# A 3x3 convolution computed by pairs of columns inside a fused convolution-and-attention kernel

## The chip, the cores and the metric

The kernel runs on one core of one Trainium2 chip. The core has five engines that run their own instruction streams: TensorE (PE in the profile; its weight loads are listed apart as PEld), VectorE (DVE), ScalarE (ACT), GpSimd (POOL) and SyncE (SP), which here only issues DMAs. Engines wait for each other through semaphores; each works through its own stream in order. The metric is the device time of one execution in microseconds (us); less is better.

## The reference, cut to what matters

Input x is 8 images of 32 x 32 positions with 256 channels, all in float32. The first layer is a group norm, then a 3x3 convolution to 192 channels beside an 8-head attention with relative positions to 64 channels. The second layer is a one-head attention over the 1024 positions and then a feed-forward part with two of eight experts per image.

```python
x = x + _L0_conv_ref(_gn(x), ...)            # 3x3 convolution (192) | attention (64)
t = _to_tokens(x)                            # (8, 1024, 256)
t = t + _L1_attn_ref(_ln_t(t), ...)          # one-head attention
t = t + _L1_ffn_ref(_ln_t(t), ...)           # top-2 of 8 experts
...
conv_out = lax.conv_general_dilated(x, conv_w, window_strides=(1, 1), padding='SAME', ...) + conv_b
```

Per image the convolution is, for each position, a sum over 3 rows and 3 columns of taps and 256 input channels.

## The kernel before

**Stages.** The program has two parts. The first (all but the last function body) goes through the 8 images and does layer 0 and the attention of layer 1; the second does the experts. One image of the first part takes about 270 us and has these stages, in TensorE's order, which is written out by hand (`tc.manual_schedule` for PE; the other engines' order is made by the scheduler of the language from priorities and dependencies):

- *Fill.* `input_steps(b + 1)` makes the next image's queries, keys, values and tables of relative positions from its normed image: products pk (L303), values pvv (L336), and 16 "small" steps of prel (L371 and L374). It is a generator; `attention_layer(b)` calls `fill` between its own steps, and `fill` runs four products of the next image's convolution behind each small step. `whole` then runs on to the end of a group.
- *Layer 1 attention* of image b: pq, lg1, tp, po1, pa1 (L673 to L759), and at its end, on GpSimd, a sum over the tokens (L793, L795) and the store of the image to DRAM (L800).
- *Score stage* of image b + 1 (`conv_layer_attention`, its first ten steps, s = 0 to 9). Each step has two scores: PE makes lg (L472), VectorE reduces it (L480), and after each second step L484 and L487 follow on VectorE. Between them stands the rest of the convolution (`conv.run(todo)`), and the generator `between`, which loads the image after (L104, on GpSimd's queue), turns it by PE (tpx, L245), copies it (L247) and takes its statistics (L248) on VectorE, adds biases on GpSimd (L252), and prepares the group norm (pm L256, pv L265). The normed image goes into `gpad` (L273).
- *Weighing stage*: scores of the later units beside exponentials (L512 on PE, L520 on ScalarE) and weighted sums po (L528). There is no convolution in it.

**The convolution** (`conv_steps`, L410 to L428). The normed image lies in `gpad` three times, shifted by one column to either side (L279 and L280 on GpSimd), with rows of zeros above and below, so that 128 positions (four rows of 32) of any tap are one contiguous piece. A tile t of 128 positions is one group of 18 products: 9 taps by 2 halves of the channels, accumulated in one PSUM bank and then added into the residual tile T by one VectorE operation (L427).

```python
lhsT=gflat[:, dx, kc, t * P + dy * WW : (t + 1) * P + dy * WW],
rhs=convw[:, i, :],
```

The bank is one of three `st` banks in the score stage, which tpx, pm, pmx and pv use too, and the only `po` bank in the fill (`place`).

An image has 8 groups, 144 products. Of these 64 run in the fill, 8 in `whole`, and 72 in the score stage (18 at its start, then 6 or 5 per step). Image 0 has no fill before it, so all its 144 run in its score stage (18, then 13 or 12 per step).

**Tokens.** T holds positions t x 128 + p in partition p, tile t; images are read, stored and written in this layout. The values of the attention lie in `v32`, 32 columns for each head (8 values, a one, and zeros).

Of the kernel before, what the change touches and what calls it, by code (L numbers as in the profile page):

```python
# [35 lines left out]
def kernel(  # L36
# [54 lines left out]
    with ExitStack() as ph:  # L91
# [9 lines left out]

        def load_image(b):
            t = work.tile([P, NT, C], FP, tag="T", name="T", bufs=2)
            nc.gpsimd.dma_start(out=t, in_=xt[b].rearrange("(t p) c -> p t c", p=P))  # L104
            return t
# [15 lines left out]
        convw = wp.tile([P, 9 * KC, CO], FP, tag="convw", name="convw")  # L121
        nc.scalar.dma_start(out=convw, in_=conv_w.rearrange("a b (k p) o -> p (a b k) o", p=P))
# [94 lines left out]

        tab = wp.tile([P, 1], FP, tag="tab", name="tab")
        v32 = wp.tile([P, NT, NH, 32], FP, tag="v32", name="v32")
        nc.gpsimd.memset(v32, 0.0)  # L220
        nc.gpsimd.memset(v32[:, :, :, DH : DH + 1], 1.0)


        gpad = wp.tile([P, 3, KC, HH + 2, WW], FP, tag="gpad", name="gpad")
        nc.gpsimd.memset(gpad, 0.0)
        gflat = gpad.rearrange("p s k h w -> p s k (h w)")
# [8 lines left out]
        def norm_steps(b):  # L235


# [3 lines left out]
            for kc in range(KC):  # L241
                for q in range(2):
                    tp = st_tile("tpx").rearrange("p (j t) -> p j t", j=4)
                    for j in range(4):
                        nc.tensor.transpose(tp[:, j, :], T[b][:, q * 4 + j, kc * P : (kc + 1) * P], ident)  # L245
                    dst = xT[:, kc, q * 512 : (q + 1) * 512]
                    nc.vector.tensor_copy(dst, tp.rearrange("p j t -> p (j t)"))  # L247
                    nc.vector.bn_stats(st[:, kc, q, :], dst)  # L248
                    yield True
                nc.vector.bn_aggr(mv[:, kc, :], st[:, kc].rearrange("p q s -> p (q s)"))  # L250
# [19 lines left out]
            yield None  # L270
            for kc in range(KC):
                xv = xT[:, kc, :].rearrange("p (h w) -> p h w", w=WW)
                nc.vector.tensor_scalar(  # L273
                    gpad[:, 1, kc, 1 : HH + 1, :], xv, gm[:, kc, :], gr[:, kc : kc + 1], ALU.subtract, ALU.mult
                )

            for kc in range(KC):
                mid = gpad[:, 1, kc, 1 : HH + 1]
                nc.gpsimd.tensor_copy(gpad[:, 0, kc, 1 : HH + 1, 1:WW], mid[:, :, 0 : WW - 1])  # L279
                nc.gpsimd.tensor_copy(gpad[:, 2, kc, 1 : HH + 1, 0 : WW - 1], mid[:, :, 1:WW])  # L280

        def by_tiles():
# [3 lines left out]
            for kc in range(KC):  # L286
                for a in range(2):
                    for e in range(4):
                        nc.gpsimd.tensor_copy(
                            xn[:, kc, a * 4 + e].rearrange("p (y x) -> p x y", y=8),  # L290
                            gpad[:, 1, kc, 1 + 16 * a : 17 + 16 * a, 8 * e : 8 * e + 8],
# [3 lines left out]
        def input_steps(b, held):  # L295
# [4 lines left out]
            for q in range(2):  # L300
                pk = st_tile("pk")
                for kc in range(KC):
# [3 lines left out]
                        rhs=gflat[:, 1, kc, WW + 512 * q : WW + 512 * (q + 1)],  # L306
# [27 lines left out]
            for j in range(NT):  # L334
# [10 lines left out]
                v32[:, :, :, 0:DH],  # L345
# [65 lines left out]
        def conv_steps(b, place):  # L411

            n = 9 * KC
            for t in range(NT):
                pc = place[0]("pc")
                for i in range(n):
                    tap, kc = divmod(i, KC)
                    dy, dx = divmod(tap, 3)
                    nc.tensor.matmul(  # L419
                        pc[:, 0:CO],  # L420
                        lhsT=gflat[:, dx, kc, t * P + dy * WW : (t + 1) * P + dy * WW],
                        rhs=convw[:, i, :],
                        start=i == 0,
                        stop=i == n - 1,
                    )
                    if i == n - 1:
                        nc.vector.tensor_tensor(T[b][:, t, 0:CO], pc[:, 0:CO], T[b][:, t, 0:CO], ALU.add)  # L427
                    yield  # L428

        class Unit:  # L430
# [91 lines left out]
            def gather(self, j, parts):  # L522
# [4 lines left out]
                for hl in range(HG):  # L527
                    nc.tensor.matmul(  # L528
                        self.po[32 * hl : 32 * hl + 32, cols],
                        lhsT=v32[:, j, self.g * HG + hl, :],  # L530
# [12 lines left out]
            def close(self):  # L543
                self.os = work.tile([P, 512], FP, tag="os", name="os")
                nc.scalar.copy(self.os, self.po)  # L545
# [21 lines left out]
        def conv_layer_attention(b, units, kq, rh, rwd, rwq, conv, between):  # L567
# [8 lines left out]
            first = min(left, 9 * KC)  # L576
            conv.run(first)
            left -= first
            for s in range(NU * NT + lead + 2):
# [34 lines left out]
                elif s == lead:  # L614
                    for _ in between:
                        pass
                if s % NT == 0 and 0 < u <= NU:
# [197 lines left out]
        class Conv:  # L815


            def __init__(self, b):
                self.place = [po_tile]
                self.steps = conv_steps(b, self.place)  # L820
                self.left = NT * 9 * KC if b < B else 0
# [7 lines left out]
            def whole(self):  # L829

                self.run(self.left % (9 * KC))

        with tc.manual_schedule(engines={mybir.EngineType.PE}):
            held = {}
            for _ in norm_steps(0):
                pass
            held["xn"] = by_tiles()
# [4 lines left out]
            for b in range(B):  # L842
                last = b + 1 == B
                def between():
                    if not last:
                        T[b + 1] = load_image(b + 1)
                    yield True
                    norm = iter(()) if last else norm_steps(b + 1)
                    while next(norm, None):
                        yield True  # L850
                    if means:
                        token_mean(*means.pop())
                    yield None
                    yield from norm

                conv.place[0] = st_tile
                conv_layer_attention(b, *(held[k] for k in ("units", "kq", "rh", "rwd", "rwq")), conv, between())
# [5 lines left out]
                def fill(us):  # L863

                    while us > 0:
# [4 lines left out]
                        if small:  # L870
                            conv.run(4)
# [156 lines left out]
    for b in range(B):  # L1028
# [22 lines left out]
        for q in range(2):  # L1051
# [34 lines left out]
            for j in range(4):  # L1086
# [5 lines left out]
                out=ot[b, q * 512 : (q + 1) * 512, :].rearrange("(t p) c -> p t c", p=P), in_=y  # L1092
# [51 lines left out]
```

## Time and profile before

| what | value |
|---|---|
| median of 3 runs | 2748.75 us (2745.79 to 2751.4) |
| profiled execution, its own time | 2752.85 us |
| span of the profiled execution, first to last instruction | 2750.8 us |
| mean granted TensorE clock | 0.970 |
| score stage of image 0, first product of the convolution to the first weighing matmul | 81.93 to 147.87 us |
| fill of image 2, first pk to the first pq | 531.06 to 581.65 us |
| score stage of image 2, first product of the convolution to the first weighing matmul | 634.21 to 686.09 us |
| load of an image, issue to landing, median of 8 | 6.3 us |

The profile is of one execution. Its page lists for each engine the busy time and its share of the span, then groups of instructions by line, engine and tile names (out<-in), with count, busy time, mean duration in ns, and the idle time of the engine just before them with what released it. A float32 matmul leaves two records, so counts of PE are twice those of the code. A timeline line gives start, length, engine, line, operation, tiles and, in brackets, how long the engine had been idle before and what ended that wait. A table by stretches gives busy times of PE, PEld, DVE, ACT and POOL in each stretch, then the granted clock (1.00 is full speed), the share of DMA and GB/s.

### The profile page before, as it was taken

The page shows a single profiled execution, that of the slowest core. Times are in us where ns is not written, and L with a number is a line of the kernel's source. Part 1 is how long each engine was busy: PE and PEld are TensorE (multiplying, and loading weights), DVE is VectorE, ACT ScalarE, POOL GpSimd, SP SyncE. Part 2 cuts the span into 40 slices and gives each one's busy share as a digit, 9 for nine tenths or more (in the row PEclk, how much of TensorE's full clock was granted, in tenths as well). Part 3 has the DMA queues.
Part 4 walks back from the last instruction along what each step waited for, and adds up shares of the span by engine and source line. Part 5 has one row for each costly group of instructions (what it writes and reads, how often), then busy time and mean ns, then how long its engine had stood idle before and what let it go on. Part 6 is the DMA issues. An engine that isn't in the chain of part 4 may idle for free.

```text
span 2750.8 us, 41933 instructions
## 1 busy us (share of the span) xinstructions
PE 2584.5 (94%) x17513; PEld 1541.4 (56%) x17513; DVE 1372.2 (50%) x2423; ACT 956.0 (35%) x1600; POOL 393.9 (14%) x440
## 2 busy tenths in 40 slices
PE   3999999999999999999999999999999859999998
PEld 2844763476347635753575367537742536666665
DVE  3474377337733773377237724862484443223332
ACT  0055215521552154315431633263336313222222
POOL 5010121002100301030103010201100131111110
PEclk9899999999999899999999999999999979999999
DMA  2330133023302320232023103320330032211110
GB/s 75 78 64 5 42 68 65 6 47 72 56 6 47 80 46 6 47 86 42 21 44 81 34 21 64 60 35 20 75 59 10 1 111 69 69 62 61 62 54 23
DMA packets 77611, 135.83 MB, mean 49 GB/s; under 512 B 12000, under 2 KB 32360, under 8 KB 75376
## 3 DMA queue, kind: packets, MB, share of 16 engines
q1 hardware_dynamic: 71504, 114.42, 19.3%
q0 software_dynamic: 3328, 16.78, 1.9%
q8 instruction: 138, 2.26, 0.3%
q10 hardware_dynamic: 2592, 1.97, 0.2%
q14 instruction: 49, 0.40, 0.1%
HBM read 53.43 MB, written 25.17 MB: 29 GB/s over the span
## 4 chain that ended last, share of the span: by engine, by line
PE 82%; DVE 8%; POOL 3%; DMA 3%; ACT 3%; issue 1%; ACTq 0%; DVEq 0%; SPq 0%; POOLq 0%
PE lg L472 13%; PE pc L419 11%; PE po L528 9%; PE py L1075 8%; PE phd L1057 8%; PE st L512 7%; PE po L741 4%; PE lg L710 3%; PE prel L371 3%; PE pq L673 2%; PE tp L730 2%; DVE my L480 2%; PE py L1072 1%; PE prel L374 1%; POOL part L793 1%; DMA T<-in_x_dram 1%
## 5 line engine op out<-in xcount | busy, mean ns | idle before, releaser
L480 DVE TENSOR_REDUCE my<-lg 128x32 f32<-128x1024 f32 x512 | 616.2, 1221 | 168.8 <-PE st L512 124.9
L520 ACT ACTIVATE PT<-st 128x512 f32<-128x512 f32 (+1 forms) x944 | 543.3, 633 | 340.7 <-PE st L512 332.7
L512 PE MATMUL st<-F,km 32*128 32x512 f32 x2048 | 549.1, 651 | 15.9 <-DMA F<-mb 15.7
L472 PE MATMUL lg<-km,F 24*128 24x512 f32 x2048 | 526.8, 656 | 1.3 <-DVE my L480 1.2
L419 PE MATMUL pc<-convw,gpad 128*128 128x192 f32 x2304 | 445.5, 343 | 6.3 <-DVE T L427 6.3
L419 PEld LDWEIGHTS pc<-convw,gpad 128*128 128x128 f32 x2304 | 381.2, 195 | 80.8 <-issue 65.1
L528 PE MATMUL po<-PT,v 128*32 128x256 f32 (+1 forms) x3200 | 314.5, 454 | 5.0 <-ACT os L545 2.6
L472 PEld LDWEIGHTS lg<-km,F 24*128 24x128 f32 x2048 | 156.1, 189 | 168.0 <-issue 105.6
L528 PEld LDWEIGHTS po<-PT,v 128*32 128x32 f32 x3200 | 67.4, 108 | 316.2 <-issue 281.5
L1075 PE MATMUL py<-w,hT 128*128 128x256 f32 x1024 | 237.3, 385 | 0.0
L512 PEld LDWEIGHTS st<-F,km 32*128 32x128 f32 x2048 | 178.2, 187 | 102.5 <-issue 64.5
L1057 PE MATMUL phd<-n2T,w 128*128 128x512 f32 x512 | 223.4, 594 | 0.0
L1075 PEld LDWEIGHTS py<-w,hT 128*128 128x128 f32 x1024 | 190.3, 190 | 45.3 <-issue 22.4
L1082 DVE TENSOR_TENSOR r<-py,n 128x256 f32<-128x256 f32 x64 | 27.2, 425 | 310.8 <-PE py L1075 310.8
L1057 PEld LDWEIGHTS phd<-n2T,w 128*128 128x128 f32 x512 | 97.0, 191 | 114.6 <-issue 107.5
L658 POOL TENSOR_TENSOR T<-T,n 128x256 f32<-128x256 f32 x64 | 47.0, 740 | 640.7 <-DVE n L653 640.7
L268 ACT ACTIVATE gr<-gr 128x2 f32<-128x2 f32 x8 | 1.6, 204 | 387.3 <-DVE gr L267 387.3
L741 PE MATMUL po<-pt,qkv 128*128 128x256 f32 x512 | 116.6, 381 | 11.3 <-DVE pt L733 11.3
L1064 ACT ACTIVATE hT<-phd,b1c 128x512 f32<-128x512 f32 x128 | 86.3, 686 | 96.3 <-PE phd L1057 96.1
L710 PE MATMUL lg<-qkv 128*128 128x512 f32 x256 | 119.1, 593 | 0.0
L741 PEld LDWEIGHTS po<-pt,qkv 128*128 128x128 f32 x512 | 96.8, 190 | 36.1 <-DVE pt L733 13.2
L719 DVE TENSOR_REDUCE nm<-lg 128x1 f32<-128x1024 f32 x64 | 78.1, 1220 | 72.5 <-PE lg L710 72.5
(220 smaller groups left out, 2456.5 us busy)
## 6 DMA issues: line engine op xcount, KB each, us to landing
F<-rh SPq DMA_DIRECT2D x256, 128.0 KB
F<-kq SPq DMA_DIRECT2D x256, 64.0 KB
F<-rwd SPq DMA_DIRECT2D x256, 64.0 KB
w<-in_L_ffn_W_dram SPq DMA_DIRECT2D x32, 512.0 KB
T<-in_x_dram POOLq DMA_DIRECT2D x8, 1024.0 KB, 6.3
rwd<-rw SPq DMA_DIRECT2D x16, 512.0 KB
Td<-T POOLq DMA_DIRECT2D x8, 1024.0 KB, 7.6
T<-Td SPq DMA_DIRECT2D x8, 1024.0 KB
```

The costliest lines, as they stand in the source:

```text
L371: nc.tensor.matmul(dst, lhsT=lhsT, rhs=kqv[rows, :, a], start=True, stop=True)
L419: nc.tensor.matmul(pc[:, 0:CO], lhsT=gflat[:, dx, kc, t * P + dy * WW : (t + 1) * P + dy * WW], rhs=convw[:, i, :], start=i == 0, stop=i = ...
L472: nc.tensor.matmul(lg[:, a, :], lhsT=self.F[r : r + 24, a, 0, i * P : (i + 1) * P], rhs=KM[self.g][r : r + 24, a].rearrange("p e k -> p (e ...
L480: nc.vector.tensor_reduce(my[:, :, hl], lg.rearrange("p a (y x) -> p y a x", y=WW), AX.XY, ALU.max)
L512: nc.tensor.matmul(st[:, i, :] if len(heads) > 1 else st, lhsT=KM[self.g][r : r + 32, a, e, :], rhs=self.F[r : r + 32, a, e, :], start=Tru ...
L520: nc.scalar.activation(self.pts[j][:, hs, :], st, AF.Exp)
L528: nc.tensor.matmul(self.po[32 * hl : 32 * hl + 32, cols], lhsT=v32[:, j, self.g * HG + hl, :], rhs=self.pts[j][:, hl, cols], start=j == 0, ...
L710: nc.tensor.matmul(lg[:, h, :], lhsT=qk[0][:, i * P : (i + 1) * P], rhs=qk[1][:, h * 512 : (h + 1) * 512], start=True, stop=True,)
L741: nc.tensor.matmul(po[:, 0:IB], lhsT=v1[:, jc, :], rhs=pt[:, jc, :], start=jc == 0, stop=jc == NT - 1)
L1057: nc.tensor.matmul(phd, lhsT=ws[k][0][:, kc, f * P : (f + 1) * P], rhs=n2T[:, kc, q * 512 : (q + 1) * 512], start=kc == 0, stop=kc == KC - 1,)
L1064: nc.scalar.activation(hT[:, k * NF + f, :], phd, AF.Gelu, bias=b1c[:, f, k * B + b : k * B + b + 1])
L1075: nc.tensor.matmul(py, lhsT=hT[:, k * NF + f, j * P : (j + 1) * P], rhs=ws[k][1][:, f, :], start=False, stop=k == TOPK - 1 and f == NF - 1,)
```

## The change

Two neighbouring columns of the output, with taps w0, w1, w2 and inputs d0 to d3, are (d0 w0 + d1 w1 + d2 w2) and (d1 w0 + d2 w1 + d3 w2): six products. They are computed from four: m0 = (d1 + d2)(w0 + w2 + w1)/2, m1 = (d2 - d1)(w0 + w2 - w1)/2, m2 = (d0 - d2) w0 and m3 = (d1 - d3)(-w2). The first column is m0 + m1 + m2 and the second m0 - m1 + m3, as the kernel has its signs.

- **Taps.** The taps are loaded into a work tile, and VectorE (four operations) and ScalarE (two) make the four sets `convw` from them once, at the start.
- **Inputs.** `gpad` is now one image with a border on all sides. A new function `by_pairs` makes the four sets `gdif` of sums and differences, 16 pairs by 34 rows each, by eight GpSimd operations of 512 elements; they take the place of the four shifted copies. It is called where the score stage ends (`behind()`, s = lead), and before `by_tiles` for image 0. The norm into `gpad` itself moves before the token mean, out of the last call of `between`.
- **Products.** A group is now one pair of sets (m0 and m1, or m2 and m3) of 128 pairs of columns (eight rows): 2 x 6 products of the same shape, 192 columns. An image has 8 groups, 96 products. The fill runs three behind each small step (48), `whole` finds nothing left to do, and 48 stand in the score stage: 12 at its start, then 4 or 3 per step. Image 0 has 12, then 9 or 8 per step.
- **Evictions.** An even group is added to T by three VectorE operations, an odd group by one of 384 elements.
- **Layout of T.** A residual tile now holds the even or the odd columns of eight rows, so two tokens that follow each other share a partition, and loads and final stores move 2 KB in one piece. The copies xT (now on ScalarE, before on VectorE) and os put tokens back in order.
- **Values.** `vall` packs 9 columns per head; a head's weight tile of 32 columns runs into the next heads' columns.

```diff
-            nc.gpsimd.dma_start(out=t, in_=xt[b].rearrange("(t p) c -> p t c", p=P))
+            nc.gpsimd.dma_start(out=t.rearrange("p (r j) c -> p r j c", j=2), in_=xt[b].rearrange("(r p j) c -> p r j c", p=P, j=2))
...
+        nc.vector.tensor_tensor(convw[:, 2], taps[:, 0], taps[:, 2], ALU.add)
+        nc.vector.tensor_tensor(convw[:, 0], convw[:, 2], taps[:, 1], ALU.add)
+        nc.vector.tensor_tensor(convw[:, 1], convw[:, 2], taps[:, 1], ALU.subtract)
+        nc.vector.tensor_scalar(convw[:, 0:2], convw[:, 0:2], 0.5, None, ALU.mult)
+        nc.scalar.copy(convw[:, 2], taps[:, 0])
+        nc.scalar.mul(convw[:, 3], taps[:, 2], -1.0)
...
-        v32 = wp.tile([P, NT, NH, 32], FP, tag="v32", name="v32")
-        nc.gpsimd.memset(v32, 0.0)
-        nc.gpsimd.memset(v32[:, :, :, DH : DH + 1], 1.0)
+        vall = wp.tile([P, NT, (NH - 1) * (DH + 1) + 32], FP, tag="vall", name="vall")
+        nc.gpsimd.memset(vall, 1.0)
...
-        gpad = wp.tile([P, 3, KC, HH + 2, WW], FP, tag="gpad", name="gpad")
+        gpad = wp.tile([P, KC, HH + 2, WW + 2], FP, tag="gpad", name="gpad")
         nc.gpsimd.memset(gpad, 0.0)
+        gdif = wp.tile([P, 4, KC, HH + 2, WW // 2], FP, tag="gdif", name="gdif")
+        nc.gpsimd.memset(gdif, 0.0)
...
-                    nc.vector.tensor_copy(dst, tp.rearrange("p j t -> p (j t)"))
+                    nc.scalar.copy(
+                        dst.rearrange("p (r t j) -> p r j t", r=2, j=2), tp.rearrange("p (r j) t -> p r j t", j=2)
+                    )
...
+        def by_pairs():
             for kc in range(KC):
-                mid = gpad[:, 1, kc, 1 : HH + 1]
-                nc.gpsimd.tensor_copy(gpad[:, 0, kc, 1 : HH + 1, 1:WW], mid[:, :, 0 : WW - 1])
-                nc.gpsimd.tensor_copy(gpad[:, 2, kc, 1 : HH + 1, 0 : WW - 1], mid[:, :, 1:WW])
+                d = [gpad[:, kc, 1 : HH + 1, j : j + WW - 1 : 2] for j in range(4)]
+                for v, (one, two, op) in enumerate(
+                    ((1, 2, ALU.add), (2, 1, ALU.subtract), (0, 2, ALU.subtract), (1, 3, ALU.subtract))
+                ):
+                    nc.gpsimd.tensor_tensor(gdif[:, v, kc, 1 : HH + 1, :], d[one], d[two], op)
...
+            n = 3 * KC
+            for r in range(NT // 2):
+                both = T[b][:, 2 * r : 2 * r + 2, 0:CO]
+                for pair in range(2):
+                    pc = place[0]("pc")[:, 0 : 2 * CO].rearrange("p (v o) -> p v o", v=2)
+                    for v in range(2):
+                        for i in range(n):
+                            dy, kc = divmod(i, KC)
+                            at = (8 * r + dy) * (WW // 2)
+                            nc.tensor.matmul(
+                                pc[:, v, :],
+                                lhsT=gflat[:, 2 * pair + v, kc, at : at + P],
+                                rhs=convw[:, 2 * pair + v, dy, kc, :],
+                                start=i == 0,
+                                stop=i == n - 1,
+                            )
+                            if v and i == n - 1:
+                                if pair:
+                                    nc.vector.tensor_tensor(both, pc, both, ALU.add)
+                                else:
+                                    nc.vector.tensor_tensor(
+                                        both, both, pc[:, 0:1, :].to_broadcast([P, 2, CO]), ALU.add
+                                    )
+                                    for j, op in enumerate((ALU.add, ALU.subtract)):
+                                        nc.vector.tensor_tensor(both[:, j], both[:, j], pc[:, 1, :], op)
+                            yield
...
                 elif s == lead:
                     for _ in between:
                         pass
+                    behind()
...
-                            conv.run(4)
+                            conv.run(3)
```

## The prediction

> **What bounds the kernel now.** I read the page's parts 1 and 5 first, then the list of what each engine waited for, then TensorE, VectorE, GpSimd and queue timelines of one image (image 2, counted from 0: 531 to 801 us), then tables by stretch of time.
>
> The page says that TensorE (PE) is busy 94% of the span and that the convolution's products are its fifth heaviest group:
>
> ```profile
> PE 2584.5 (94%) x17513; PEld 1541.4 (56%) x17513; DVE 1372.2 (50%) x2423; ACT 956.0 (35%) x1600; POOL 393.9 (14%) x440
> ...
> L419 PE MATMUL pc<-convw,gpad 128*128 128x192 f32 x2304 | 445.5, 343 | 6.3 <-DVE T L427 6.3
> ```
>
> One matmul leaves two records, so 2304 records are 1152 products (144 per image, 8 images). Back to back one costs 5.85/18 = 0.325 us (36 records in 5.85 us in the chain of work); a run of four after another kind costs 1.50. After the change there are 96 per image. "94% busy" says that 48 products x 8 images x 0.325 = 125 us come off; I don't believe it, because the products stand in two different stages. From the table by stretches (columns: length, busy us of PE, its weight loads, VectorE, ScalarE, GpSimd, then the granted clock):
>
> ```profile
> 531.00:582.00 51.00, 50.10 (x595) 43.50 (x594) 15.14 (x39) 8.91 (x14) 10.39 (x9) 1.00 0.08 27
> ...
> 634.00:657.40 23.40, 22.82 (x137) 17.42 (x135) 16.11 (x25) 0.70 (x2) 13.95 (x17) 1.00 0.63 151
> 657.40:688.00 30.60, 27.00 (x131) 18.35 (x134) 26.73 (x41) 1.49 (x2) 4.83 (x2) 0.80 0.11 24
> ```
>
> In the first stretch ("fill": the next image's convolution between small matmuls of layer 1) PE is the only full engine. The other two are the "score" stage (20 reduces, the rest of the convolution, the next image's norm). After 657.4 VectorE is full (26.7 of 30.6), PE waits, and its clock falls to 0.80. The timelines show why:
>
> ```profile
> 657.38 0.66 PE L245 MATMUL tpx<-ident,T 128*128 128x128 f32 x4 [0.58 <-DMA T<-in_x_dram]
> ...
> 676.78 0.58 PE L256 MATMUL pm<-gmv,gavg 128*128 128x2 f32 x2 [3.58 <-DVE gmv L250]
> ```
> ```profile
> 667.79 2.34 DVE L480 TENSOR_REDUCE my<-lg 128x32 f32<-128x1024 f32 x2
> 670.16 4.30 DVE L484 TENSOR_TENSOR my<-my,rwq 128x128 f32<-128x128 f32 x1
> ```
> ```profile
> 669.82 4.49 POOL L252 TENSOR_TENSOR T<-T,l0b 128x2048 f32<-128x2048 f32 x1 [18.20 <-PE tpx L245]
> ```
> ```profile
> 672.00:675.00 3.00, 1.20 (x8) 0.90 (x6) 2.93 (x4) 0.00 (x0) 2.31 (x1) 1.00 0.00 0
> 675.00:678.00 3.00, 1.22 (x6) 0.98 (x6) 2.93 (x7) 0.00 (x0) 0.00 (x0) 0.60 0.00 0
> 678.00:681.00 3.00, 3.00 (x10) 1.08 (x8) 2.65 (x7) 0.00 (x0) 0.00 (x0) 0.50 0.00 0
> ...
> 690.00:693.00 3.00, 3.00 (x15) 1.97 (x11) 1.43 (x2) 1.39 (x3) 1.99 (x3) 0.55 0.70 118
> ```
>
> Three things are to be seen. The first transpose of the next image (tpx) already waits 0.58 for its load. L484, else 0.29, takes 4.30 while GpSimd's L252 runs beside it; behind it PE waits 3.58 for gmv. After that wait the clock is 0.5 until about 691. All six images that norm a next one after image 0 show it, 7 to 17 us long.
>
> **The change, part by part**
>
> *Fill, seven times (images 1 to 7).* Before: 16 runs of four (24.0) + 8 in one run (2.6) + two waits of 0.45 for the single po bank = 27.5. After: 16 runs of three, 1.50 - 0.325 = 1.175 each, 18.8. What is late next is the po bank. A group is now 12 products = 4 small steps, so it always ends at a step's end, and the next group comes after prel and tpn (1.02 + 0.31) in the first eight steps, after 0.60 in the others. An even group is emptied by three VectorE operations instead of one. L427 (192 elements) is 0.355 and L498 (512) 0.685, so 384 elements are 0.55: 0.55 + 2 x 0.355 = 1.26, behind a copy of prel (1.07 or 0.69) and with one n (0.41) in between. That ends 1.9 and 1.5 after the group's last product, so PE waits about 0.65 and 0.9 once each; an odd group (0.55) is hidden. 27.5 - 18.8 - 1.6 = **-7.1 each, -50 in all**. Bounds: -8.7 each with no wait, -4 if each of the four groups waits 1.2.
>
> *Score stage of images 1 to 6.* 24 products fewer are 24 x 0.34 = 8.2 us less for PE. Count from the stage's first product (634.21). Before, tpx comes 23.2 later. After: 12 products 3.9; then each of five steps runs at VectorE's pace (2.36 for two reduces + half of 0.67 for L484 and L487 = 2.7, plus evictions), and PE is at tpx about 18.5 after the start. The load isn't there: GpSimd's sum of tokens runs 637.09 to 650.63, the load is issued behind it on the same queue and takes 6.3 to 6.7; all of it starts from the end of the stage before, and nothing of it is shortened. (Two tokens per partition, 2 KB in one piece, may help; I take 0 to 1 us.) So PE now waits 4 to 5 us where it waited 0.58, and 4.7 of the 8.2 are gone. From tpx on VectorE decides: busy 27.5 before; without four copies (now on ScalarE, idle here) -2.7; evictions of the two groups that end here 1.26 + 0.55 for 2 x 0.355, +1.1; so 25.9, **-1.6**. Against it: a 3.58 wait was followed by half clock for 7 to 17 us, and the new wait is longer. At half clock a step is 2.1 (scores) + 2.8 (four products) + 1.1 (tpx) = 6.0 on PE against 3.9 on VectorE; over 8 us that costs 2 to 3. The old wait at pm stays, since L252 still meets a two-input operation. I take **0 each**. Bounds: -4.5 (no half clock, earlier load) to +4 (14 us of half clock).
>
> The row behind this is the one above: 3.58 us of wait, clock 0.5 until 691. [...]
>
> *Image 0's score stage* has all its products: 81.93 to 147.85, 65.9 us, PE full. After: 96 x 0.335 = 32.2, 20 scores 10.7, transposes and small ones 3.6, the wait for F (now 12 products instead of 18 cover it) about 4: 50.5. VectorE: reduces 23.6, L484/L487 3.4, seven evictions 6, norm 6.6, GpSimd meeting 2 to 3, start 4: 46. Both are near, and each waits for the other now and then: I take 55, **-11** (bounds -15 and -4).
>
> *Start of the program.* VectorE forms sums of taps ahead of bdh: three operations of 1152 elements (from 0.685 for 512 and 1.22 for 1024, 1.36 each) and one of 2304 (L273: 0.77 for 1024, so 1.7): 5.8. ident's followers, reld and km on GpSimd go 5 to 6 later, but the 5.5 us memset of gpad, which held gpad until 43.99, now runs in GpSimd's empty time before 21 us. Then GpSimd must do l0b (4.5), the eight differences and the x copies (4.3) in this order. A difference of 512 elements, from 0.74 for 256 and 4.49 for 2048, is 1.28: 10.2, where four copies were 4.5. pvv's last operand comes at about 61.5 instead of 57.7. **+2.3** (bounds -4, +8).
>
> *Image 7's score stage* has no norm behind it; VectorE's pace rules: the first run is 6 products shorter, **-2** (bounds -4, 0).
>
> *Differences on GpSimd in images 1 to 7*, 10.2 at the start of the weighing stage: their reader comes some 90 us later, so they are hidden; but L484 may wait for one, 1.28 at most, three times, and VectorE has 0.6 us of slack per step: **+0.5 each, +3.5** (bounds 0, +10).
>
> *At nothing*: the shorter weight tile of the attention (same matmul shapes), ScalarE's reordering copies (L545, 0.59 before; +0.3 at each of 32 if reading in steps costs, +10), the output in pieces of 2 KB (hidden behind the expert stage's PE).
>
> Sum: -49.7 + 0 - 11 + 2.3 - 2 + 3.5 = **-57**. The profiled execution took 2752.85 (span 2750.8); it becomes 2696. The median of the runs shown is 4.1 lower (2748.75), so I forecast **2692**.
>
> **Rivals**
>
> 1. *PE alone counts*: every product saved is time, 2749 - 125 = 2624. For it: 94% busy. Against: VectorE's 26.73 of 30.60 and the load that already makes tpx wait. Chance 0.07.
> 2. *The clock holds* after the new wait, or the load lands earlier: score stages -4 each, -24 more: 2668. For it: in three of six images the half clock lasted only 7 to 8 us. Chance 0.22.
> 3. *The forecast*, 2692: 0.45.
> 4. *Evictions and waits eat more*: fill -4 each (+22), score +3 each (+18): 2732. For it: the single po bank and VectorE as the bound. Chance 0.15.
> 5. *Slower: half clock runs on.* Place: from the tpx wait into the weighing stage, where PE is full (84.00 of 84.00). Price: half the time spent at 0.5. It decides when an image spends 19 us more at half clock than before (9.5 lost x 6 = 57); 30 us more give 2692 + 90 = 2782. Against: PE is dense there, and the longest stretch seen is 17. Chance 0.08.
> 6. *It doesn't do what it says*: PE reads the padded, stepped rows or the new groups slower and products cost 0.49 instead of 0.325: near 2749. Nothing in the trace shows it. Chance 0.03.
>
> **How the numbers follow.** Cases 2, 3 and 4 hold 0.82; the range runs from a little below case 2 to case 4: 2650 to 2735. About 0.2% is what a measurement of this kernel tells from no change. Faster: cases 1 to 4, 0.89; same: 0.03; slower: 0.08.
>
> **What would show it.** Right: 1536 records of the convolution; a fill of about 44 us instead of 51; PE waiting 4 to 5 us for the load at the first tpx of images 2 to 7, with half clock after it; score stages of images 1 to 6 near 52 us as before; image 0's near 55. Wrong: a score stage of 47 or less, no wait at tpx, VectorE idle after it, po waits over 1.2 us, or a longer fill.

## The result and the profile after

Before: median 2749.81 us (2738.98 to 2756.49, 20 runs). After: median 2774.67 us (2736.19 to 2817.98, 20 runs). The ratio after/before is 1.0033 [1.0014, 1.0053]. A third fewer products, and the kernel is not faster: by the ratio it is the same within 2%, by the medians 25 us slower. The times of the changed kernel scatter over 82 us where those of the kernel before scatter over 18; the ratio leaves out the ten highest runs, among them the profiled execution (2786.8 us, span 2784.9).

From the page of the changed kernel, engine row and the convolution's group:

```profile
PE 2587.9 (93%) x16745; PEld 1510.3 (54%) x16745; DVE 1389.6 (50%) x2459; ACT 981.2 (35%) x1635; POOL 427.5 (15%) x472
...
L447 PE MATMUL pc<-convw,gdif 128*128 128x192 f32 x1536 | 371.0, 393 | 5.7 <-DVE T L462 5.7
```

The records are the 1536 foretold, but the mean of one rose from 343 to 393 ns, and PE is as busy as before (2584.5) with 768 records fewer. Something else makes PE slow. Stage lengths, from the first matmul of a kind to the first of the next (PE timelines of both kernels):

| stages, summed | before | after | difference | forecast |
|---|---|---|---|---|
| start to image 0's first weighing matmul | 147.9 | 148.6 | +0.8 | -8.7 |
| fill, images 1 to 7 | 359.0 | 380.0 | +20.9 | -50 |
| score, images 1 to 6 | 306.3 | 293.2 | -13.1 | 0 |
| score, image 7 | 40.5 | 45.9 | +5.4 | -2 |
| weighing, all eight | 924.0 | 943.8 | +19.8 | +3.5 |

The rest differs by less than 1 us. The fills hold the biggest miss. Four of the seven last 42.6 us, three last 69.9. The table by stretches (length; busy us of PE, its weight loads, VectorE, ScalarE, GpSimd; granted clock, DMA) has a fill of each kind, and then the second half of a score stage and the start of the weighing stage behind it:

```profile
524.27:566.85 42.58, 41.43 (x545) 35.53 (x545) 16.51 (x42) 8.59 (x14) 10.39 (x9) 1.00 0.10 33
781.49:851.37 69.88, 69.50 (x546) 59.92 (x545) 16.47 (x42) 9.11 (x14) 10.37 (x9) 0.56 0.06 20
...
926.00:954.21 28.21, 23.66 (x105) 15.22 (x105) 23.48 (x34) 2.93 (x6) 4.49 (x1) 0.75 0.05 11
954.21:975.00 20.79, 20.79 (x145) 8.27 (x144) 15.55 (x19) 12.00 (x21) 8.76 (x8) 0.85 0.59 90
```

Both fills hold the same work (545 and 546 matmul records). The one difference is the column before the DMA share: clock 1.00 and 0.56. "PE busy 69.50 of 69.88" hides it, since the same matmuls are busy longer at half clock (16 records of prel in the lines below: 1.09 us at 788.65, 1.92 at 792.23). The timeline of the long fill shows where the clock goes, in the very first small step:

```profile
785.04 3.68 PE L359 MATMUL pvv<-qkvw,x 128*128 128x64 f32 x32
788.65 1.09 PE L394 MATMUL prel<-kq,bdw 32*128 32x32 f32 x16
789.67 2.21 PE L447 MATMUL pc<-convw,gdif 128*128 128x192 f32 x6
791.67 0.63 PE L697 MATMUL tpn<-ident,n 128*128 128x128 f32 x2
792.23 1.92 PE L394 MATMUL prel<-kq,bdw 32*128 32x32 f32 x16
794.08 2.29 PE L447 MATMUL pc<-convw,gdif 128*128 128x192 f32 x6
```

No line has a wait in brackets: PE never stands still here, yet from 789.8 three products take 2.2 us where a short fill has

```profile
532.45 1.24 PE L447 MATMUL pc<-convw,gdif 128*128 128x192 f32 x6
```

All changes of the clock in the traces of the two kernels lie multiples of 3.413 us apart; the pieces between such marks are called windows here. The 3.41 us before the drop and the 3.41 us behind it, PE busy in all of both:

```profile
786.38:789.79 3.41, 3.41 (x38) 3.30 (x38) 2.19 (x7) 1.70 (x3) 0.00 (x0) 1.00 0.07 14
789.79:793.20 3.41, 3.41 (x18) 2.99 (x18) 0.72 (x2) 0.00 (x0) 1.80 (x3) 0.50 0.12 25
```

In the kernel before, the same drop happens behind pvv in two of seven fills (a third fill starts with 3.4 us at half clock under pk), but there it ends after one stretch of 3.4 us:

```profile
269.45:272.86 3.41, 3.41 (x14) 2.98 (x12) 0.44 (x2) 0.00 (x0) 1.50 (x2) 0.50 0.12 24
272.86:276.30 3.44, 3.44 (x40) 3.20 (x42) 0.83 (x2) 0.00 (x0) 0.84 (x2) 1.00 0.12 24
```

In the changed kernel it lasts 61.4 us, to 0.14 us before the end of the fill at 851.37; the last window holds the fill's last three products and tpw, and no prel. A long fill costs 27.3 us, and the runs (2736, 2753 to 2767, 2782 to 2798, 2815 to 2818) lie in clusters about that far apart, which fits one to four long fills. Their mean granted clocks (0.939, 0.927 to 0.932, 0.914 to 0.920, 0.906 to 0.907) fit too: 61.4 us at half clock are 30.7 lost of some 2780, 0.011 of the mean. Only one run was traced. Without its three, the profiled execution would be 2786.8 - 82 = 2705.

Two of the forecast waits are there as well, as PE, VectorE and GpSimd timelines of image 3's score stage show:

```profile
926.55 1.11 PE L263 MATMUL tpx<-ident,T 128*128 128x128 f32 x4 [3.43 <-DMA T<-in_x_dram]
...
946.26 0.35 PE L276 MATMUL pm<-gmv,gavg 128*128 128x2 f32 x2 [3.94 <-DVE gmv L270]
```
```profile
939.94 4.64 DVE L519 TENSOR_TENSOR my<-my,rwq 128x128 f32<-128x128 f32 x1
```
```profile
939.94 4.49 POOL L272 TENSOR_TENSOR T<-T,l0b 128x2048 f32<-128x2048 f32 x1 [18.68 <-PE tpx L263]
```

tpx waits for the load (3.4 to 3.6 us in six images, 20.6 in all); behind it VectorE's correction starts with GpSimd's long addition and ends with it, and pm waits 3.94. The clock is at half for 6.8 us after the first and for 13.7 after the second, into the weighing stage. Summed over the part with the eight images, 2250 us, the changed kernel runs 416 us at half clock, the kernel before 160.

### The profile page after: what moved, and what is told of

It is laid out like the page before. It is cut to its first block, busy times and chain, and to the rows that moved or that the text cites. A ratio compares the mean times of both kernels' runs of the same rounds, so it can differ in the third digit from the quotient of the medians.

```text
span 2784.9 us, 40526 instructions
## 1 busy us (share of the span) xinstructions
PE 2587.9 (93%) x16745; PEld 1510.3 (54%) x16745; DVE 1389.6 (50%) x2459; ACT 981.2 (35%) x1635; POOL 427.5 (15%) x472
## 3 DMA queue, kind: packets, MB, share of 16 engines
q1 hardware_dynamic: 67408, 114.42, 19.8%
## 4 chain that ended last, share of the span: by engine, by line
PE 81%; DVE 8%; POOL 4%; DMA 3%; ACT 3%; issue 1%; SPq 0%; ACTq 0%; DVEq 0%; POOLq 0%
PE lg L507 13%; PE po L564 9%; PE pc L447 8%; PE py L1112 8%; PE phd L1094 8%; PE st L547 8%; PE po L781 4%; PE lg L750 3%; PE prel L394 3%; PE pq L713 2%; PE tp L770 2%; DVE my L515 2%; POOL part L833 2%; PE prel L397 1%; PE py L1109 1%; DMA T<-in_x_dram 1%
## 5 line engine op out<-in xcount | busy, mean ns | idle before, releaser
L547 PE MATMUL st<-F,km 32*128 32x512 f32 x2048 | 563.4, 670 | 17.0 <-DMA F<-mb 16.4
L507 PE MATMUL lg<-km,F 24*128 24x512 f32 x2048 | 555.0, 683 | 1.9 <-DVE my L515 0.7
L447 PE MATMUL pc<-convw,gdif 128*128 128x192 f32 x1536 | 371.0, 393 | 5.7 <-DVE T L462 5.7
L447 PEld LDWEIGHTS pc<-convw,gdif 128*128 128x128 f32 x1536 | 301.8, 226 | 82.8 <-issue 71.8
L564 PE MATMUL po<-PT,vall 128*32 128x256 f32 (+1 forms) x3200 | 319.4, 461 | 3.9 <-ACT PT L555 2.4
L507 PEld LDWEIGHTS lg<-km,F 24*128 24x128 f32 x2048 | 162.7, 195 | 177.3 <-issue 105.0
L564 PEld LDWEIGHTS po<-PT,vall 128*32 128x32 f32 x3200 | 67.7, 109 | 322.4 <-issue 289.0
L1112 PEld LDWEIGHTS py<-w,hT 128*128 128x128 f32 x1024 | 189.9, 190 | 45.6 <-issue 22.4
L593 DVE RECIPROCAL rc<-pa 128x16 f32<-128x16 f32 x32 | 8.3, 258 | 207.3 <-PE pa L590 207.3
```

Source lines behind the costliest of these rows:

```text
L447: nc.tensor.matmul(pc[:, v, :], lhsT=gflat[:, 2 * pair + v, kc, at : at + P], rhs=convw[:, 2 * pair + v, dy, kc, :], start=i == 0, stop=i ...
L507: nc.tensor.matmul(lg[:, a, :], lhsT=self.F[r : r + 24, a, 0, i * P : (i + 1) * P], rhs=KM[self.g][r : r + 24, a].rearrange("p e k -> p (e ...
L547: nc.tensor.matmul(st[:, i, :] if len(heads) > 1 else st, lhsT=KM[self.g][r : r + 32, a, e, :], rhs=self.F[r : r + 32, a, e, :], start=Tru ...
L564: nc.tensor.matmul(self.po[32 * hl : 32 * hl + 32, cols], lhsT=vall[:, j, h * (DH + 1) : h * (DH + 1) + 32], rhs=self.pts[j][:, hl, cols], ...
L1112: nc.tensor.matmul(py, lhsT=hT[:, k * NF + f, j * P : (j + 1) * P], rhs=ws[k][1][:, f, :], start=False, stop=k == TOPK - 1 and f == NF - 1,)
```

## Experiments

Each ratio is to the kernel before, run on the same chip at the same time, with a 95% interval.

**1. The same products in the fill, six behind every second small step**

```diff
+                turn = [0]
...
-                            conv.run(3)
+                            turn[0] += 1
+                            if turn[0] % 2 == 0:
+                                conv.run(6)
```

> The changed kernel with the same 48 products per fill, but six behind every second small step instead of three behind each. Theory A (a dropped clock comes back only in a stretch of about 3.4 us that is nearly full of large products; three products at half clock are 2.2 us between small matmuls, six are 4.2 us): no fill stays at half clock, every fill is 42 to 47 us, mean clock 0.95 or more, the times lie together near 2705 (2786.8 of the profiled run less 3 x 27.3 for its three long fills), within 15. Theory B (the share of large products in the fill decides, and it is unchanged) and theory C (the new operands lower the clock, for instance the weight columns of the attention values that were zeros): fills of 70 us in some images as in the changed kernel, times scattered between 2736 and 2818, mean clock 0.90 to 0.94.

Measured: 2732.9 us (2721.36 to 2735.14), 0.994 [0.992, 0.996]. The fills take 42.1 to 48.7 us and none stays at half clock (3.4 to 17.1 us each, no piece over 6.9). The third one, which took 69.9 us in the changed kernel's trace:

```profile
797.14:839.27 42.13, 41.63 (x546) 36.79 (x545) 16.86 (x42) 8.91 (x14) 10.38 (x9) 0.96 0.10 33
```

Same products, same count, other packing: theory A holds for the fill in that six win the clock back and three do not; how full a stretch must be for it is not shown. The total misses the 2705 expected by 28 us. In the trace, of a run of 2721.4 us, the seven fills take 308 instead of 298, and score stages 1 to 6 take 301 instead of the 293 of the changed kernel's trace, with 20.5 us at half clock from the end of most of them into weighing; the other 12 us lie between this run and the median of its eight.

**2. The kernel before with three products per step instead of four**

```diff
-                            conv.run(4)
+                            conv.run(3)
```

> The kernel before with three products instead of four behind each small step of the fill; the rest of its 144 products moves into the score stage (90 instead of 72 there). Theories A and B (three products per step are too thin): in some of the seven fills the clock stays at 0.5 to the end, these fills take 65 to 75 us, the mean clock falls to 0.92 to 0.95, the times scatter by steps of about 25 us and lie above 2760. Theory C (the new operands or tiles are the cause): clock 0.97 as before, no fill at half clock for more than about 7 us, times within 10 us of each other between 2735 and 2765.

Measured: 2870.36 us (2814.54 to 2899.34), 1.0301 [1.0241, 1.0362]. All seven fills of its trace take 71.6 us, each 61.4 us of it at half clock. The first of them:

```profile
259.02:330.62 71.60, 71.60 (x557) 62.09 (x557) 14.56 (x37) 9.20 (x14) 10.35 (x9) 0.57 0.06 19
```

The old products in the old layout do the same, so neither the new operands nor the new evictions are the cause: it is the thin step.

**3. The changed kernel with four products per step**

```diff
-                            conv.run(3)
+                            conv.run(4)
```

> The changed kernel with four products behind each small step, as the kernel before had: 64 in the fill, 8 more to the end of the group, 24 left in the score stage. Theories A and B: no fill at half clock for more than about 7 us, fills of 50 to 53 us, mean clock 0.95 or more, times together near 2740 (2705 plus 7 x 8 for the longer fills, less about 20 from shorter score stages). Theory C: long fills remain (over 75 us), times scatter.

Measured: 2794.66 us (2785.24 to 2808.44), 1.0181 [1.015, 1.0213]; a miss of 55 us. The fill is at full clock, as theory A says, but with the eight that `whole` adds to end a group it takes 24 products more from the score stage, which has 24 left, two or one per step, and loses the clock itself; a fill and a stretch across score and weighing:

```profile
533.49:584.86 51.37, 49.37 (x594) 43.34 (x594) 18.09 (x46) 8.92 (x14) 10.40 (x9) 1.00 0.08 27
...
645.00:703.00 58.00, 52.36 (x184) 23.97 (x182) 41.05 (x55) 9.49 (x16) 22.24 (x21) 0.53 0.32 65
```

54.6 us at half clock from the waits at tpx and pm into the weighing stage, which takes 120.2 us instead of the 113 to 115 of the kernel before. That is the mechanism of rival 5, at its place, in a kernel with a thinner score stage.

**4. Experiment 1, with the long addition on GpSimd in eight pieces**

```diff
-            nc.gpsimd.tensor_tensor(T[b], T[b], l0b.to_broadcast([P, NT, C]), ALU.add)
+            for t in range(NT):
+                nc.gpsimd.tensor_tensor(T[b][:, t, :], T[b][:, t, :], l0b[:, 0, :], ALU.add)
```

> As the run with six, and GpSimd adds the biases of layer 0 in eight pieces of 256 elements instead of one of 2048. Theory D (the one long GpSimd addition holds VectorE's two-input operation, PE waits at pm, and the clock halves at the end of the score stage): L519 is never above 1.1 us, the wait at pm falls from 3.9 to under 1 per image, score stages of images 1 to 6 shorten by 3 to 5 us each and the start of the weighing stages loses its half clock, together 20 to 40 us less than the run with six. Rival E (VectorE is the bound, the wait only moves to the next score): score stages change by less than 1.5 us each, total within 10 us.

Measured: 2691.86 us (2680.3 to 2701.98), 0.9797 [0.9765, 0.9828]. VectorE's correction in one image, and the four pieces of GpSimd's addition that run beside it:

```profile
396.83 0.53 DVE L520 TENSOR_TENSOR my<-my,rwq 128x128 f32<-128x128 f32 x1
```
```profile
396.48 2.85 POOL L273 TENSOR_TENSOR T<-T,l0b 128x256 f32<-128x256 f32 x4 [1.21 <-PE tpx L263]
```

0.53 instead of 4.64; the wait at pm goes in all six images, and the score stages fall from 50.2 to 44.4 us, so that a wait of 3.9 us had cost some 6. The gain of 41 us in the medians is just above the 20 to 40 expected (28 us between the two traced runs). One part of theory D failed: the half clock at the start of the weighing stages stays, 10 to 17 us each, and these stages take 957 us in all instead of 943. In the changed kernel VectorE's correction and GpSimd's addition both began at 939.94 and ended within 0.2 us of each other (4.64 and 4.49 us); in this run the correction takes 0.53 beside pieces of 0.71 on average: its length goes with that of the one GpSimd instruction beside it.

**5. The kernel before, with that edit alone**

> The kernel before, with one edit: GpSimd adds l0b to the next image in eight operations of 256 elements instead of one of 2048. Theory D (the long addition holds up VectorE's maximum correction, 4.30 us instead of 0.29 us, and PE waits 3.58 us for gmv behind it, then runs at half clock): the correction falls to about 0.3 us, the wait at pm to under 0.6 us, and the six score stages lose about 4 us each (PE is busy 49.8 of some 54 us there, so not more than 5): 2749 - 25 = 2724, between 2714 and 2734. If that is so, the six_split kernel's gain owes nothing to the pairs of columns and has to be compared with this kernel. Rival (the score stage is held by PE's products in this kernel, so the addition is hidden): score stages unchanged at about 51 us and a time within 5 us of 2749.

Measured: 2714.49 us (2713.58 to 2715.18), 0.9867 [0.9847, 0.9886]. The stretch from the first tpx to the end of image 2's score stage (in the kernel before 657.40 to 686.09; its row to 688.00 has clock 0.80) is here

```profile
650.00:672.86 22.86, 22.39 (x127) 14.62 (x125) 22.16 (x38) 0.00 (x0) 5.60 (x8) 1.00 0.02 5
```

PE is busy 22.4 of 22.9 us at full clock; the score stages take 45.3 instead of 50.2 to 51.9. So the wait at pm was never part of the change, and kernels that have the addition in pieces are to be compared with 2714, not 2749.

**6. The changed kernel, with eight more products among the pairs of pvv**

```diff
                         if small:
                             conv.run(3)
+                        elif took < 0.5 and conv.left > 88:
+                            conv.run(1)
```

> The changed kernel, still three products behind each small step of the fill, but eight more products (taken out of the next score stage, with the four that fill up the group) stand among the pairs of pvv's small matmuls, one behind each pair. Theory A2 (the clock is lost in the stretch of pvv and first prel, which has no product in it; three products per step hold full speed but cannot win it back): no fill runs at half clock for more than 7 us; the fill is 42.6 + 12 x 0.33 = 46.5 us in all seven; the time is 2705 + 28 for the products moved here - 0 to 12 in the score stages that are thinner = 2715 to 2735, and the runs lie within 10 us of one another. Rival A1 (three products per step lose the clock by themselves, wherever the fill begins): some fills are still 60 us and over, the clock falls at some place behind the first step, and the time stays over 2745 with a scatter of 30 us and more.

Measured: 2931.43 us (2919.11 to 2937.81), 1.0643 [1.0606, 1.068]: theory A2 fails as it stood. The first step runs at full clock, but eight products leave a group that ends inside the second (the next expectation says the third, wrongly), PE waits there for the po bank, and from then on the clock is half, in all seven fills (75.6 to 77.3 us). PE timeline and stretch of one:

```profile
569.88 1.60 PE L447 MATMUL pc<-convw,gdif 128*128 128x192 f32 x4 [1.39 <-DVE T L462]
```
```profile
569.90:632.00 62.10, 59.41 (x471) 50.93 (x472) 8.48 (x15) 5.97 (x9) 8.14 (x6) 0.51 0.05 19
```

**7. The same with twelve, so that a group ends with pvv**

```diff
+                        elif took < 0.5 and conv.left > 84:
+                            conv.run(1 + conv.left % 3 // 2)
```

> As the run with eight more products in pvv, with twelve, so that a group ends with pvv's last pair and no group ends in the middle of a step; the first product of the fill's first step then waits at most 0.7 us for the po bank (there it was 1.39 in the third step, and the clock fell behind it in all seven fills). Theory A3 (a window that holds the bare pvv and prel, or a wait of more than 1 us, loses the clock; three products a step, with waits of 0.4 to 0.8 as in the changed kernel, hold it at full speed): no long fills, fill 46.5 us in all seven, time 2715 to 2735. Rival A1 (three products a step are too thin at full speed too, and it is chance whether a window falls badly): some fills still run at half clock, from some step on, and the time is over 2750.

Measured: 2737.34 us (2733.39 to 2739.01), 0.9952 [0.9937, 0.9967]. All seven fills take 46.5 us at full clock, and the runs lie within 6 us; the total is 2 us above the range. PE timeline and stretch:

```profile
543.42 1.21 PE L447 MATMUL pc<-convw,gdif 128*128 128x192 f32 x6 [0.43 <-DVE T L462]
```
```profile
530.80:577.30 46.50, 45.44 (x569) 39.30 (x569) 17.32 (x44) 8.58 (x14) 10.38 (x9) 1.00 0.09 30
```

In these traces three products a step held full clock (all seven fills here, four in the changed kernel) and did not win it back (61.4 us at half clock in each of its other three); it was lost behind pvv's 64 columns and prel with no product among them, or behind the wait of 1.39 us in experiment 6. A3 stands.

**8. Experiment 4, with an early load**

The load of the image after the next is issued ahead of GpSimd's sum of tokens, into a free buffer of the `pt` pool, and GpSimd's eight additions read that buffer and write T.

```diff
+            src = X.pop(b) if b else T[0]
...
+            if b + 2 < B:
+                load_early(b + 2)
             acc = work.tile([P, C], FP, tag="n", name="acc", bufs=2)
```

> The six_split kernel (fill in runs of six behind every second step, l0b added in eight pieces), with the load of the image after the next issued before GpSimd's sum of tokens, into a buffer of the size of an image that is free from the end of layer 1 on; GpSimd then adds l0b out of that buffer into T. Theory E (the wait for the load, 20.5 us in six images, and the half clock behind it stand on the path): the wait at tpx falls below 1 us, the score stages of images 1 to 6 from 44.4 to 39.5 to 41.5 us, the half clock at their place goes, and the time falls by 20 to 32 us to 2660 to 2672 when six_split takes 2692. Rival F (VectorE, busy 36 of 43 us there, decides, and the time lost at tpx is taken back by its backlog): the wait goes, the stages lose under 1.5 us each, time 2683 and over.

Measured: 2658.07 us (2650.08 to 2664.2), 0.9661 [0.9631, 0.9691]. On the PE timeline the first tpx has no wait:

```profile
376.86 0.60 PE L270 MATMUL tpx<-ident,X 128*128 128x128 f32 x4
```

Score stages 39.0 (one 40.0) instead of 44.4: 5.4 each for a wait of 3.5. Theory E stands, with stage and total a little under its ranges; F fails. The weighing stages stay at 117.4: their half clock isn't the load's.

**9. Experiment 8, with the token mean of the last image called later**

```diff
+                    else:
+                        for _ in range(3):
+                            yield True
                     if means:
                         token_mean(*means.pop())
```

> The kernel of the early load, and besides the last image's token mean put back behind the fourth further step of its score stage, as in the kernel before (the changed kernel calls it at the second step, where PE waits 6.2 us for GpSimd's sum). If that wait is what made the last score stage 45.9 us instead of 40.5, the stage falls to 40 to 41.5 us and the time by 4.5 to 6 us against the early load alone: about 2660. Rival (the longer stage comes from the thinner products): the stage stays over 44 us.

The three `yield`s put the mean behind the seventh step of the stage (s = 6). The kernel before has it behind the fifth (s = 4), so this is later than its old place, which the expectation names; both are behind GpSimd's sum.

Measured: 2645.4 us (2639.3 to 2648.49), 0.9613 [0.9589, 0.9638]. PE timelines of image 7's score stage, experiment 8 and then this one:

```profile
1896.78 1.01 PE L859 MATMUL pmt<-ones,acc 128*128 128x1 f32 x4 [6.24 <-POOL acc L847]
```
```profile
1900.15 0.50 PE L859 MATMUL pmt<-ones,acc 128*128 128x1 f32 x4
```

That stage falls from 45.5 to 37.8 us, more than expected; the total falls by 12.7, of which some 5 are not in that stage and are not explained.

**10. Experiment 9, with products of the score stage held back to its last two steps**

```diff
+            held_back = left == 36
...
-                    todo = -(-left // (lead - s))
+                    todo = (3 if s < lead - 2 else 6) if held_back else -(-left // (lead - s))
```

> The kernel with the early load and the early mean, and its 36 products of the score stage's steps shared out otherwise: three in each of the first eight steps and six in each of the last two, instead of four, four, ... three. Theory G (the clock is lost at the end of the score stage, 642 to 656 us, because three products a step leave the small matmuls pm, pmx, pv and pmt thinly covered there): the 10 to 14 us of half clock at the start of the weighing stages of images 1 to 6 go in most of them, these stages fall from 117 to 119 to 113.5 to 115 us, and the time by 15 to 30 us to 2615 to 2630. Rival H (the rows of 24 and 32 of the scores themselves lose it, where they stand alone at the start of weighing): the half clock stays, the time within 8 us of 2645.

Measured: 2616.92 us (2605.01 to 2622.85), 0.9504 [0.9458, 0.9549]. The passage from score to weighing, experiment 9 (642.2) and then this one (648.8), by stretches:

```profile
643.00:648.00 5.00, 5.00 (x22) 3.35 (x21) 3.73 (x4) 3.27 (x5) 4.11 (x4) 0.56 0.61 121
648.00:653.00 5.00, 5.00 (x18) 0.92 (x11) 3.35 (x4) 2.28 (x4) 4.54 (x5) 0.50 0.72 123
```
```profile
648.00:653.00 5.00, 4.83 (x28) 2.13 (x27) 4.93 (x10) 3.66 (x6) 2.72 (x3) 1.00 0.59 130
653.00:658.00 5.00, 5.00 (x40) 1.63 (x40) 4.14 (x6) 3.06 (x6) 5.00 (x6) 1.00 0.68 115
```

PE has no wait in the first pair; the half clock there is a thin end of the score stage, and six products in each of the last two steps, the same number in all, remove it. The weighing stages of images 1 to 6, 113.4 to 119.6 us in experiment 9 (two of them at 113.4), are now all between 113.1 and 114.2. Theory G stands, H fails. This is the fastest kernel of the study; against experiment 5 the pairs of columns, with their products placed as in experiments 1 and 10, the load as in 8 and the mean as in 9, are worth 2714 - 2617 = 97 us, of the 125 that PE's count alone says. The placing, the early load and the later mean were not tried on the kernel before, so what they would give there is not measured; in experiment 5 image 2 is at clock 1.00 from its score stage into weighing (627.63 to 688.00).

## Why the prediction was wrong

The forecast was 2692 in 2650 to 2735; the median is 2775.

- **The fill (-50; it became +20.9).** The step that failed is "PE is the only full engine", with 1.175 us for each run of three: a price at full clock, for work that gets thinner. At full clock it holds: 42.6 us against a forecast of about 44, -8.0 per fill where I had -7.1, and the po bank makes PE wait 0.35 and 0.79 (0.65 and 0.9 forecast). But three of seven fills lose the clock and cost 27.3 each, 82 us; seven fills of 42.6 would have come to -61. I had read the half clock as something that a wait brings. The trace shows that it comes without one (PE busy 3.41 of 3.41 us before the drop at 789.8), experiments 1 and 2 that the size of a run decides whether it goes (with six no piece at half clock over 6.9 us, with three 61.4 in each fill), and experiment 7 that the bare stretch of pvv and prel brings it (with products in it none of seven fills lost the clock, without them three of seven).
- **Score stages 1 to 6 (0; it became -13.1).** Right in kind: the wait at tpx was 3.4 to 3.6 us (4 to 5 forecast), half clock follows (6.8 us in image 3), and the wait at pm stays (3.94 there). They end 2.2 us better on average (44.7 to 50.3), inside the bounds.
- **Weighing (+3.5; it became +19.8).** I had priced GpSimd's differences here. The clock is the cause: stretches of up to 23.9 us at half clock that begin at the end of the score stage and reach up to 19 us into this one. Experiments 4 and 8 took both waits away and the stages stayed near 117 to 120; experiment 10, which moves only products, brought them to 113 to 114. So rival 5 (0.08) had the mechanism, and its trigger only in part: besides the wait, too few products around the small matmuls. Its place did not decide the result: from score into weighing an image has 12.5 us more at half clock than before, and rival 5 needed 19. No rival named the fill.
- **Image 0 and the start (-8.7; it became +0.8).** The first product of the convolution comes 6.1 us later (+2.3 forecast), and the stage behind it is 5.4 us shorter (-11 forecast). Why is not settled. In its trace pvv waits 5.5 us for GpSimd's copies x, where before it waited 0.37 (GpSimd makes the differences first), and half clock then lasts 34 us instead of 20; no run separates the two.
- **Image 7's score stage (-2; it became +5.4).** I had not followed the moved `yield`s: for the last image the token mean comes at the second step instead of the fifth, ahead of GpSimd's sum (6.25 us of waiting). Experiment 9 shows it: with the mean later, the wait goes and the stage takes 37.8 us.

The sign was lost in the first of these. The count of what would show it named "a longer fill" among the signs against the forecast; the reason for one was in the trace of before, in two fills that drop to half clock behind pvv for 3.4 us, which I missed because I had looked at one fill alone (531 to 582), and that is one without a drop.

## What to carry to other kernels

Here the work taken out of a stretch of small matmuls was also what kept the clock up: in the trace of before, with four products a step, a drop in a fill ended after 3.4 us, in that of the changed kernel, with three, it lasted 61.4. Before removing such work, look at the granted clock in pieces of some 3 us over every repeat of the stage, not at one repeat, and ask how much of such a piece is left. If it is little, three placings won time here: the rest in longer runs (six instead of three, experiment 1), among the small matmuls (experiment 7), and at the end of a stage (experiment 10). A gain that is missing in the total can still be there for the most part: here 97 of 125 us, hidden by a clock, a load and a moved call, beside a long GpSimd instruction that both kernels had.

## What the runs showed of the hardware

- **The clock falls without a wait.** From 786.38 to 789.79 PE was busy 3.41 of 3.41 us, with only pvv (64 columns) and prel (32 x 32) from 785.04 on, and the clock went from 1.00 to 0.50 (changed kernel). The stretches at half clock that end in the two kernels' part with the eight images are 3.4, 6.8, 10.2, 13.7, 17.1, 20.5, 23.9, 34.1 and 61.4 us, all multiples of 3.413. What a window counts is not shown.
- **What won it back.** At half clock a step of three products is 4.50 us (792.23 to 796.73): prel 1.85, products 2.08, tpn 0.57. In the three long fills 51 windows, 17 in a row in each, held 1.56 to 2.64 us of products and tpn, 46 to 77%, and the next was still at half clock; the 18th held 3.31 to 3.41 us of products and tpw, and full clock followed. With four, both drops behind pvv in the trace of the kernel before ended after one window: the one from 269.45 to 272.86 held some 3.3 us, 96%, but the one from 1883.95 to 1887.36 held 2.65 (products 2.09, tpn 0.56), 78%. So 77% did not win it back and 78% did; that this share alone draws the line is not shown. Six products are 4.2 us at half clock (twice 2.08), more than a window. The shares are estimates from the rows; that prel counts for little is inferred, not shown by itself.
- **One step, two outcomes.** With the same program some fills lost the clock and some didn't (three and four of seven), and its runs scatter by 82 us; with twelve products in pvv, where no fill of the trace lost it, they scatter by 6. It goes with where a window's edge falls: the 14 fills in the traces of the two kernels have the same bare pvv and prel, 4.63 us long. In five of them a window began between 1.20 and 1.55 us after pvv's first matmul, and all five had half clock from the end of that window on; in the nine others (the nearest began at 1.08 and 1.59) none did. In the trace of experiment 2 the half clock of the first three fills begins at 267.5, 557.6 and 847.7, some 290.1 us or 85 windows apart (estimated from its clock in stretches of 2.5 us), and all seven of its fills lost the clock.
